# Graph attention over 16 batches on one core: a plan with separate steps for two early tables, the long rows, the pieces and the last batch

## Chip, cores, metric

One core of one Trainium2 chip. The metric is the device time of one execution in microseconds (us); lower is better. "Span" is the time from the first to the last instruction of the one execution that was profiled.

## The reference, cut to what matters

```python
# x: (16, 1024, 512); adj: (1024, 1024), 0/1, ones on the diagonal; biases are zero
h = jnp.maximum(_layernorm(x, axis=-1), 0.0)
q, k, v = (h @ W + b for each of Wq, Wk, Wv)      # 8 heads of 64
scores = einsum('bihd,bjhd->bhij', q, k) / 8 + where(adj == 0, -1e9, 0)
out = einsum('bhij,bjhd->bihd', softmax(scores), v)
return x + out.reshape(b, n, 512)
```

The adjacency matrix is sparse and the same for all batches. The rows have very different numbers of neighbours: many in the first rows, few in the last.

## The kernel before

The kernel sorts the rows by their number of neighbours, so that tile 7 (the last 128 rows in that order) needs only 2 gathered rows per row and tile 0 needs 11 or more. Rows of tile 0 that have still more get extra rows, "pieces" of four neighbours. For each batch it

- loads x in sorted order (an indirect load on GpSimd), normalises (VectorE, GpSimd, ScalarE), transposes and projects it (TensorE), and stores K and V as a table in DRAM;
- gathers rows of K and V in "units" of 2 to 4 (indirect loads on GpSimd; the row's own K and V on SyncE), multiplies them with the queries and sums each head (VectorE), takes the exponential and weighs V (ScalarE), and folds (VectorE, GpSimd) or accumulates (TensorE).

Batch 0 has a **prologue** ahead of it that makes the permutation ("perm"), the lists of neighbours and the slots. The order of all instructions is fixed before the kernel is built: every operation is entered in a plan with an engine, an estimated length and a "place" (a priority), and a list scheduler simulates the engines and buffers and writes down the order it finds. A place is therefore not a position. What comes out depends on everything that is in the plan.

```python
# the prologue in the plan: one table carries the permutation, the norms' scales and the lists
for t in range(NT):
    add(("list_of", t), "DVE", 2.5, -43.18 + t, [("ends",), ("no_diagonal", t)], [sources])
    add(("spread", t), "POOL", 1.35, -40 + t, [("list_of", t), ("shift", (t - NT) // 2)], delay=2.5)
add(("collect",), "SP", 0.05, -31, [("spread", t) for t in range(NT)], delay=3.0)
add(("perm_of",), "DVE", 0.2, -31, [("collect",)])
add(("spots",), "DVE", 2.1, -25, [("collect",)])
add(("long_rows",), "POOL", 1.35, -23.08, [("perm_of",)], [("g", -2)], 4.5, 1.5)
add(("longest", -1), "DVE", 1.25, -4, [("long_rows",)], [sources, ("g", -2)])
for k in range(ROUNDS):
    add(("longest", k), "DVE", 2.5, -0.28 + 0.5 * k, [("longest", k - 1)], [("g", -2)])
add(("pieces",), "DVE", 9.0, 2.19, [("longest", ROUNDS - 1)], [("pht", "pieces"), ("g", -2)], delay=1.0)
add(("slots", 0), "DVE", 0.7, 5, [("pieces",), ("spots",)])
# ... cut: x, norms, projections, stores; then for each unit i of all batches:
    add(slot, "POOL", 1.35, i - 4.33 + 0.1 * s, stored, [g], delay=4.0, moves=1.5)      # gather
    add(("multiply", i), "DVE", 0.15 + 0.533 * count, i, slots + [q_of[q]], [g, q])
    add(("score", i), "DVE", 0.15 + 0.533 * count, i - 0.31, [("multiply", i)], [g])
    add(("exponent", i), "ACT", 0.22, i + 0.15, [("score", i)])
# ... cut

def spread(t):                      # eight scatters into one DRAM tile
    nc.gpsimd.indirect_dma_start(
        out=table[:], out_offset=on(ap=spot_i[:, t : t + 1], axis=0), in_=before[:, t, :], in_offset=None
    )

def longest(k):                     # eight more neighbours per round, always over 1024 columns
    row = LONG[0][:, 0, :]
    # ... cut: two passes that mark the neighbours, for k < 0
    nc.vector.max(found0[:, ts(k, 8)], row)
    if k < ROUNDS - 1:
        nc.vector.match_replace(row, found0[:, ts(k, 8)], row, 0.0)

def slots(later):                   # indices for the gathers, and how many slots are free
    c = slice(split, SLOTS) if later else slice(0, split)
    nc.vector.tensor_scalar(index[:, c], spot[:, c], -1.0, float(N), op0=ALU.mult, op1=ALU.add)
    free = once.tile([P, SLOTS], F32, tag="free", name=f"free_{later}")
    nc.vector.tensor_scalar(free[:, c], spot[:, c], 0.0, -1.0, op0=ALU.is_equal, op1=ALU.mult)
    for t in range(1, NT) if later else (-1, 0):
        # ... cut: first, end
        number = once.tile([P, 1], F32, tag="number", name=f"number_{t}")
        nc.vector.tensor_reduce(number, free[:, first:end], AX.X, ALU.add)
        nc.vector.tensor_copy(weights[:, end, :], number.to_broadcast([P, H]))
    # ... cut

# after main_path: the check of all row sums, in a pool that is opened behind the last output
with tc.tile_pool(name="c_sb", bufs=1) as pool:
    all_rows_fine(tc, pool, sums, cover, fine)
```

## Time and profile before

| | kernel before |
|---|---|
| time: the 3 runs known to the prediction; these and a fourth, in the rounds with the changed one | 1815.95 to 1825.46, median 1818.92; 1809.92 to 1825.46, median 1817.43 |
| span of the profiled execution, mean granted clock | 1806.0 us, 0.959 |
| first multiply of batch 0, of batch 1, of batch 15 | 112.3, 244.0, 1704.8 us |
| beat: (1704.8 - 244.0) / 14 | 104.3 us a batch |
| first multiply of batch 15 to the end | 101.2 us |

The three numbers "first multiply of batch 1", "beat" and "last batch" cut the span into prologue with batch 0, pipeline and tail: 244.0 + 14 x 104.34 + 101.2 = 1806.0. The times are the starts of VectorE's first K times Q product of a batch, read from the timeline.

This is the timeline of ScalarE in the prologue of the kernel before (start, length in us, engine, line, operation, in brackets how long it sat idle and what ended that):

```profile
114.93 0.58 ACT L610 COPY hT<-pht 128x512 f32<-128x512 f32 x1 [16.02 <-remote]
119.19 0.58 ACT L610 COPY hT<-pht 128x512 f32<-128x512 f32 x1 [3.68 <-remote]
```

ScalarE copies transposes (pht) that TensorE has made. TensorE's transposes ended at about 101 us by the trace, and ScalarE starts at 114.9. "Remote" means that the view found no instruction that released it.

### The profile page before, as it was taken

What the parts mean: (1) busy time and instruction counts of PE and PEld (TensorE: products, weight loads), DVE (VectorE), ACT (ScalarE), POOL (GpSimd) and SP (SyncE); (2) the same over time, 40 slices, a digit from 0 to 9 for tenths busy, and PEclk for the clock granted to TensorE, in tenths of its full rate; (3) what the DMA queues carried; (4) which work ended last, traced back from release to release, by engine and by line L of the source; (5) the groups of instructions that cost most, each with busy time, mean ns of one, the idle gap of its engine ahead of it and who ended that gap; (6) DMA issues with size and microseconds to landing.
All of it is one profiled execution on the core that took longest, in us unless ns stands there. A gap on an engine that the chain in (4) does not pass through costs nothing. (4 is left out here: it accounts for less than half of the span.)

```text
span 1806.0 us, 19695 instructions
## 1 busy us (share of the span) xinstructions
PE 1643.0 (91%) x4301; PEld 756.7 (42%) x4301; DVE 1560.5 (86%) x1883; ACT 1495.7 (83%) x5557; POOL 1322.7 (73%) x1230
## 2 busy tenths in 40 slices
PE   6959899898999989899999989899898989999895
PEld 3424344443444444444444444344444444444331
DVE  5567888989889898989889898988988998898995
ACT  4236988998898889988889988989898899889964
POOL 4445668878787887778688777878777777877773
PEclk9969989999999999999999999999999999999997
DMA  5375888889898888989889898988889898998983
GB/s 210 115 260 189 315 301 305 321 292 340 294 350 308 310 323 297 335 303 335 300 317 330 293 332 293 337 322 318 318 302 324 299 333 311 323 337 294 331 308 134
DMA packets 151781, 539.97 MB, mean 299 GB/s; under 512 B 18908, under 2 KB 18908, under 8 KB 151656
## 3 DMA queue, kind: packets, MB, share of 16 engines
q0 software_dynamic: 111888, 399.09, 61.4%
q1 hardware_dynamic: 39768, 139.56, 21.5%
q8 instruction: 36, 0.59, 0.1%
q14 instruction: 89, 0.73, 0.1%
HBM read 437.85 MB, written 100.72 MB: 298 GB/s over the span
## 5 line engine op out<-in xcount | busy, mean ns | idle before, releaser
L829 ACT ACTIVATE g<-g,weights 128x64 f32<-128x64 f32 x4768 | 1181.1, 338 | 15.6 <-DVE weights L816 6.9
L793 POOL DMA_INDIRECT g<-kv,index x624 | 631.7, 1012 | 208.2 <-issue 154.1
L615 PE MATMUL pq<-wq,hT 128*128 128x512 f32 x1024 | 463.8, 596 | 0.0
L615 PE MATMUL pk<-wk,hT 128*128 128x512 f32 x960 | 443.5, 605 | 11.5 <-ACT hT L610 9.2
L803 DVE TENSOR_TENSOR g<-g,pq 128x2048 f32<-128x2048 f32 (+2 forms) x208 | 397.8, 1913 | 39.3 <-PE pq L615 19.0
L615 PE MATMUL pv<-wv,hT 128*128 128x512 f32 x960 | 431.6, 592 | 0.0
L807 DVE TENSOR_REDUCE weights<-g 128x32 f32<-128x2048 f32 (+2 forms) x224 | 430.9, 1924 | 0.7
L834 DVE TENSOR_TENSOR g<-g 128x512 f32<-128x512 f32 (+1 forms) x285 | 286.5, 1009 | 20.9 <-ACT g L829 17.4
L615 PEld LDWEIGHTS pq<-wq,hT 128*128 128x128 f32 x1024 | 196.0, 191 | 225.9 <-issue 222.0
L615 PEld LDWEIGHTS pk<-wk,hT 128*128 128x128 f32 x960 | 186.1, 195 | 231.4 <-issue 203.5
L615 PEld LDWEIGHTS pv<-wv,hT 128*128 128x128 f32 x960 | 182.4, 190 | 214.4 <-issue 211.3
L896 POOL DMA_INDIRECT out_dram<-x,perm x128 | 149.3, 1167 | 97.8 <-DMA out_dram<-x,perm 46.1
L563 POOL DMA_INDIRECT x<-in_x_dram,perm x128 | 145.9, 1140 | 39.5 <-issue 31.0
L852 PE MATMUL acc<-g,ident 128*128 128x512 f32 x176 | 102.4, 699 | 70.2 <-POOL g L834 63.7
L834 POOL TENSOR_TENSOR g<-g 128x512 f32<-128x512 f32 x105 | 139.8, 1331 | 31.9 <-DVE g L834 15.4
L598 ACT ACTIVATE h<-x,shift,rstd 128x512 f32<-128x512 f32 x120 | 91.0, 805 | 46.5 <-DVE shift L588 42.0
L605 PE MATMUL pht<-ident,h 128*128 128x128 f32 x512 | 88.5, 314 | 40.2 <-issue 20.4
L626 ACT COPY kvt<-pk 128x512 f32<-128x512 f32 x120 | 69.0, 575 | 59.4 <-issue 21.2
L823 DVE TENSOR_TENSOR g<-g,weights 128x512 f32<-128x512 f32 (+1 forms) x149 | 108.5, 728 | 1.3 <-issue 0.9
L605 PEld LDWEIGHTS pht<-ident,h 128*128 128x128 f32 x512 | 70.9, 165 | 85.3 <-issue 44.5
L893 POOL TENSOR_TENSOR x<-x,o 128x512 f32<-128x512 f32 x68 | 87.7, 1290 | 24.2 <-DVE o L884 22.0
L610 ACT COPY hT<-pht 128x512 f32<-128x512 f32 x128 | 72.1, 578 | 37.6 <-remote 19.7
(221 smaller groups left out, 1161.7 us busy)
## 6 DMA issues: line engine op xcount, KB each, us to landing
g<-kv SPq DMA_DIRECT2D x128, 512.0 KB
kv<-kvt SPq DMA_DIRECT2D x120, 512.0 KB
g<-kv,index POOLq DMA_INDIRECT x624
adj<-in_adj_dram SPq DMA_DIRECT2D x8, 512.0 KB
x_first<-in_x_dram SPq DMA_DIRECT2D x8, 256.0 KB
x<-in_x_dram,perm POOLq DMA_INDIRECT x128
out_dram<-x,perm POOLq DMA_INDIRECT x128
wk<-in_L_gnn_Wk_dram SPq DMA_DIRECT2D x1, 1024.0 KB
```

The costliest lines, as they stand in the source:

```text
L563: nc.gpsimd.indirect_dma_start(out=X[n][:], out_offset=None, in_=x_rows, in_offset=on(ap=perm[:, t : t + 1], axis=0), element_offset=b * N * D
L598: nc.scalar.activation(HN[n], X[n], AF.Relu, bias=shift, scale=scale)
L605: nc.tensor.transpose(PH[n][:, c, :], hn[:, ts(c, P)], ident)
L615: nc.tensor.matmul(pt, HT[n][:, c, :], W[name][:, c, :], start=False, stop=(c == DC - 1))
L793: nc.gpsimd.indirect_dma_start(out=G[i][:, s].rearrange("p j d -> p (j d)"), out_offset=None, in_=KV[b % len(KV)][:], in_offset=on(ap=inde ...
L803: nc.vector.tensor_tensor(k, k, Q[b, t][:, None, :].to_broadcast([P, count, D]), ALU.mult)
L807: nc.vector.tensor_reduce(weights[:, w, :], heads(G[i][:, :count, 0, :]), AX.X, ALU.add)
L823: nc.vector.tensor_tensor(v, v, own.to_broadcast([P, n, H, HD]), ALU.mult)
L829: nc.scalar.activation(v[:, h, :], v[:, h, :], AF.Identity, scale=weights[:, c + s, h : h + 1])
L834: engine.tensor_tensor(v[:, 0:n], v[:, 0:n], v[:, first : first + n], ALU.add)
L852: nc.tensor.matmul(ACC[b, home], owner_t if t < 0 else ident, v[:, s, :], start=(u == parts_of(home)[0] and s == 0), stop=(u == parts_of(h ...
L896: nc.gpsimd.indirect_dma_start(out=out_rows, out_offset=on(ap=perm[:, t : t + 1], axis=0), in_=X.pop(b * NT + NT - 1 - t)[:], in_offset=No ...
```

## The change

The intent, part by part: the permutation and the norms' scales leave in a small table of their own ("told"), ahead of the lists, and each of the two tables is split over two DRAM tiles in turn, so that a scatter no longer waits for the one just before it; long rows are searched in 16 blocks of 64 columns and only the best of each block in rounds; the pieces become eight operations that the plan can place one by one; all places and lengths are set anew; the last batch runs from tile 0 to tile 7; the check gets tiles of its own, so that it need not wait for the pipeline's.

```diff
-        add(("spread", t), "POOL", 1.35, -40 + t, [("list_of", t), ("shift", (t - NT) // 2)], delay=2.5)
-    add(("collect",), "SP", 0.05, -31, [("spread", t) for t in range(NT)], delay=3.0)
+        behind = lambda name: [(name, t - 2)] if t > 1 else [("zeros",)]
+        add(("tell", t), "POOL", 1.3, -35.76 + 0.3 * t, [("ranks",), ("shift", (t - NT) // 2)] + behind("tell"), delay=2.0)
+        add(("spread", t), "POOL", 1.3, -36.45 + t, [("list_of", t)] + behind("spread"), delay=2.0)
+    add(("collect", "told"), "SP", 0.05, -39, [("tell", t) for t in range(NT)], delay=2.6)
+    add(("collect", "lists"), "SP", 0.05, -31, [("spread", t) for t in range(NT)], delay=2.6)
... (cut: loads reordered, x before the adjacency; count_pieces ... pieces as plan operations)
-        add(("norm", n), "ACT", 0.81, p - 4.41, [("shift", n // 2) if b else ("load_x", n)], [("x", n), ("h", n)])
-        add(("flip", n), "PE", 0.50, p - 4.02, [("norm", n)], [("h", n), ("pht", n)])
+        add(("norm", n), "ACT", 0.81, p - 5.50, [("shift", n // 2) if b else ("load_x", n)], [("x", n), ("h", n)], delay=0.00)
+        add(("flip", n), "PE", 0.62, p - 4.32, [("norm", n)], [("h", n), ("pht", n)])
... (cut: some forty places and lengths of this kind)
+        i = b * NU + (LAST_ORDER.index(u) if b == B - 1 else u)
...
-            add(("add_up", i), "PE", 0.88 * (1 if folds(b, B, count) else count), i + 0.33, weighed, [g, acc])
+            add(("add_up", k), "PE", 0.88 * (1 if folds(b, B, t, count) else count), i + 0.84, weighed + ([("add_up", k - 1)] if u != parts[0] else []), [g, acc])
...
+        def scatter(name, t):
+            nc.gpsimd.indirect_dma_start(
+                out=tables[name][t % 2][:], out_offset=on(ap=spot_i[:, t : t + 1], axis=0), in_=before[name][:, t, :], in_offset=None
+            )
...
+            for c in range(4 * k - 4, 4 * k):
+                block = row.rearrange("p (k c) -> p c k", c=blocks)[:, c, :]
+                got = LONG[0][:, 1, most * c : most * (c + 1)]
+                nc.vector.max(got[:, 0:8], block)
+                nc.vector.match_replace(block, got[:, 0:8], block, 0.0)
+                nc.vector.max(got[:, 8:16], block)
...
-    with tc.tile_pool(name="c_sb", bufs=1) as pool:
-        all_rows_fine(tc, pool, sums, cover, fine)
+    all_rows_fine(tc, keep, sums, cover, fine)
```

## The prediction

> **What bounds the kernel now.** I read the busy table by stage first, because an average over stages with different limits says little. Stage table of the kernel before (stretch, its length, busy us and instruction count of each engine, granted clock, DMA share, GB/s):
>
> ```profile
> 75.00:100.00 25.00, 21.46 (x58) 10.32 (x57) 16.10 (x39) 8.35 (x13) 16.62 (x17) 0.86 0.60 195
> 100.00:125.00 25.00, 4.42 (x23) 3.50 (x22) 17.60 (x27) 5.17 (x8) 13.49 (x15) 0.60 0.97 373
> ...
> 400.00:800.00 400.00, 375.87 (x991) 172.56 (x990) 361.19 (x418) 356.59 (x1347) 312.03 (x285) 0.98 0.88 319
> ```
>
> There are three stages. From about 240 us to 1700 us the sixteen batches run as a pipeline in which four things are nearly full: TensorE 94%, VectorE 90%, ScalarE 89%, DMA 88%. Before that lies a prologue in which almost nothing is full. From 100 to 125 us TensorE works 4.4 of 25 us. After it lies a tail. The start times of the first multiply of each batch (the K times Q product, VectorE L803), read from the timeline, give the beat: batch 1 starts at 244.0 us, batch 15 at 1704.8, so one batch takes (1704.8-244.0)/14 = 104.3 us. Batch 0 starts at 112.3 and so takes 131.7, over 27 us more than a normal one.
>
> Next, the list of waits (waiting instruction, who released it, total us, times, longest):
>
> ```profile
> PE acc L852 <- POOL g L834: 64.1, 16, 8.1
> ...
> DVE sums L874 <- ACT weights L811: 52.6, 33, 13.8
> ...
> DVE g L803 <- PE pq L615: 19.0, 30, 1.9
> ```
>
> In the pipeline TensorE stops once a batch for some 4 us at the first accumulation of tile 0, waiting for the fold on GpSimd. VectorE stops for row sums whose exponentials are not there, and at the first multiply, whose query projection stands behind a K projection. In the stretch 655 to 1596 us, nine batches, VectorE is busy 93.8 us of a batch (mean of five batches) and waits some 10.6: sums 2.5, pq 1.7, shift 1.9, o 1.3, gathered and loaded rows 1.5, others. TensorE is busy 99.5 us. So neither is full: they wait for each other in turn, by a fixed order.
>
> Third, the timeline of the prologue:
>
> ```profile
> 65.78 1.23 DVE L662 MAX8 before<-adj 128x8 f32<-128x1024 f32 x1
> 80.58 0.17 DVE L673 CAST perm<-after 128x8 int32<-128x8 f32 x1 [13.57 <-DMA after<-table]
> ...
> 131.75 0.18 DVE L874 TENSOR_REDUCE sums<-weights 128x8 f32<-128x24 f32 x1 [13.84 <-ACT weights L811]
> ```
>
> VectorE is done with the lists at 67 us and sits idle 13.6 us until the permutation arrives. The cause is on GpSimd: eight scatters into one table, each 2.88 us after the last (61.33 to 75.72 in five steps), though issuing one takes 0.96. With the permutation at 80.6 the loads of x start, the last K/V store goes out at 93.13, the first gathers at 98.2 and 99.45. The second gap, 13.84 us, follows 16.0 and 3.7 us in which ScalarE waited for TensorE's transposes; the view names no releaser ("remote"), and I can't say what it is.
>
> Last, the chain that ended last (start, us, what):
>
> ```profile
> 1793.79 2.75 DMA out_dram<-x,perm
> ...
> 1796.71 1.22 DVE c_both L1025
> 1797.93 1.13 DVE c_both L1026
> ```
>
> The final check begins only when the last output has landed; it runs to 1800.26, and the span ends at 1806.0.
>
> **What the Trainium skill says.** "DMA: Bandwidth & Descriptors", section "Anatomy of one DMA", gives each transfer on the GpSimd path about 2 us of fixed cost, mostly the receipt of the write. The trace agrees: 2.88 us per dependent scatter less 0.96 of issue leaves 1.92. "VectorE: DVE Perf Modes", section on the TRN2 errata, gives a one-input-rate fp32 operation (N+151)/0.96 ns. The trace agrees: 1024 wide 1.22 to 1.23 us against 1.22, 512 wide 0.68 to 0.69. "TensorE: Matmul & The Clock Gate", section "The HAM clock gate", says an idle TensorE falls to half clock; the trace shows 0.60 in 100-125 us. "Perfetto Trace Analysis", section "Identifying the Most-Contended Engine", warns that matmul busy share is no measure of headroom; I therefore don't read 94% as a floor.
>
> **The change, part by part.**
> 1. Two early tables in alternating DRAM tiles. The permutation no longer travels with the lists. Its eight scatters need only the ranks (44.3 us before) and the norms' scales. In the instruction order of the changed kernel they are mixed with K/V stores and the first four lists: sixteen GpSimd issues up to the last one, of which the fourth list is the latest to be ready. Lists start at about 47 us (before 47.8; transposes of the keys come some 2.5 us sooner since x tiles 0 and 1 are loaded and normalised first; one extra 1.2 us operation is put before the lists). Fourth list 47+4x2.39 = 56.6, then two or three issues of 1.25: last scatter about 59.5, landed 61.5, read back at 64.5. On VectorE the permutation stands after the eighth list, about 66.3. So the permutation comes at about 66.8 instead of 80.6: 14 us sooner. But K/V of batch 0 needs 16 projections of 3.65 us on TensorE, which was busy throughout (last one ended at 84.7) and starts only 2.5 us sooner: 82.5 to 84. What is won here is the delay behind it: eviction was at 88.7 because ScalarE stood at a norm whose x came late, and the store at 93.1. Now eviction and store can go at about 84.5, then three x loads, first gathers at about 89. That is 10 us, not 14.
> 2. Long rows by blocks. Before: two passes, ten MAX8 of 1.22, nine replacements of 1.30 = 26.4 us of VectorE, the last at 149.6. After: one pass of 1.23, sixteen blocks of three 64-wide operations, 0.22 us each by the formula plus 0.08 for the value load, 0.74 a block = 11.9, then nine rounds on 256 wide, 0.42 twice and 0.08 = about 8. About 21 us, an estimate: only 5 us less work. The gain is in place: the buffer of the long row is free at about 100 us and not at 153, where the gathers of unit 5 (152.7) waited.
> 3. Pieces as separate operations. Before, one block from 153.2 to 160.5 with waits of 3.8 and 0.7 us of VectorE for TensorE, and slots at 166.5. After, they lie before the first multiply. Worth about 5 us.
> Together: first multiply at about 101 (before 112.3), first exponential at about 104 (before 131.5), the second batch at about 104+107 = 211 (before 244), 33 us sooner at best. The unnamed 16 us wait may come back, as the same transposes and norms alternate; I give it half a chance of 10 to 12 us. Prologue: -27.
> 4. The new places in the pipeline. The set of instructions per batch stays (109 on VectorE in both orders). But on TensorE the first two query projections now come right after the transposes of the next batch, ahead of the K projection; from the tile 0 accumulation to a ready query it was 0.9+0.15+1.2+0.8+3.65+3.65 = 10.3 us, now 5.9. Row sums of VectorE stand one or two operations later, scales' shifts get more distance. That addresses pq 1.7, sums 2.5, shift 1.9 of the 10.6 us of waits; I take half, 3 us of a batch. TensorE's busy 99.5 includes overlap of issue, its work is 24x3.65+4.4+0.9+3.8 = 96.7, so 101.3 is possible. 14 to 15 batches: -43.
> 5. Last batch from tile 0 to 7, check apart. From the last score to landed output was 1784.8 to 1796.5 = 11.8 us (12 accumulations on TensorE, scale, residual). With the two-row unit last: exponential, sums, share 0.9, weighing 2.0, fold 0.7, residual on VectorE 0.7, output 3.1 = 7.4. The check's 3.6 us now run beside the output. Tail: -7.
> Sum: 1818.9-27-43-7 = 1742.
>
> **The rivals.** (a) The pipeline keeps its beat, because it is held by transfers or TensorE. For it: DMA share is 0.88 and would be 0.91, all engines are within 5%. Against: in 1650-1750 us DMA ran at 0.92 to 0.93 and 331 GB/s. Then only 34 us come, 1785. (b) The earlier permutation makes x loads, eight more scatters, and gathers collide: DMA is at 0.97 in 100-125 us already. Then the gathers start earlier but land as late, batch 0 gains 10 rather than 27: 1759 with the rest. (c) TensorE becomes the bound and the waits on it grow: period stays at 103, sum 1765. (d) The unnamed wait vanishes and VectorE's waits mostly go, period 99.5: 1705.
>
> **Range and chances.** The prologue may give 10 to 35, the beat 0 to 70 (weight on 25 to 55), the tail 4 to 9. That gives 1742 with 1705 to 1785. Two per cent is 1782.5, reached if prologue and tail come in full even with hardly any gain in the beat. Faster 0.91, same 0.08, slower 0.01.
>
> **What would show it right or wrong.** The cast of the permutation near 67 us; the first indexed gather near 89; the first exponential near 104; the second batch's first multiply near 211; distance between batches 101 to 102 us; waits of VectorE on sums and pq well under 52.6 and 19.0; the check's reductions over before the last output has landed. The step most likely to be wrong is the beat: if the distance is still 104, the order was not what held it. Next is the 16 us wait of ScalarE.

## More of the kernel before

Kernels that were sent together ran on one chip and share the runs of the kernel before. I call the three groups of experiments **chip A** (kernel before: median 1804.95 us), **chip B** (1814.89) and **chip C** (1793.94). Which chip the first pair of profiles came from is not recorded.

## The result, and the profile after

| | before | after |
|---|---|---|
| median of the runs of the same rounds | 1817.43 (4 runs) | 1770.20 (1770.12 to 1773.76, 4 runs) |
| span, clock | 1806.0, 0.959 | 1768.2, 0.971 |
| first multiply of batch 0 | 112.3 | 128.1 |
| first multiply of batch 1 | 244.0 | 234.6 |
| beat | 104.3 | (1675.0 - 234.6) / 14 = 102.9 |
| last batch to the end | 101.2 | 93.2 |

The ratio of after to before is 0.9744 (95% interval 0.970 to 0.979). A ratio is the mean time of one kernel's fast runs over that of the other's of the same rounds, so it is not quite the ratio of the medians in the table. The change is faster; I had predicted 1742 (-77 us) and it is 1770 (-47). The time is inside the range, and some 30 us of the expected gain are missing. By the cut of the spans, the prologue gave -9.4 where I wrote -27, the pipeline 14 x -1.46 = -20 where I wrote -43, and the tail -8.0 where I wrote -7. These add up to -37.8, the difference of the spans; the medians differ by 47, since the profiled execution of before was a quick one for its kernel (1807.72 us).

One thing in this cut is not like for like: the changed kernel starts its last batch with tile 0, so "first multiply of batch 15" is another instruction in it, and the step from batch 14 to 15 took 101.4 us before and 105.6 after. Over batches 1 to 14, where it is the same instruction, the beat fell from 104.6 to 102.7 us, and from the first multiply of batch 14 to the end it was 202.5 us before and 198.7 after. So the tables here give some 4 us too little to the pipeline and too much to the tail.

The stage table after, to be held against the one in the prediction:

```profile
75.00:100.00 25.00, 14.82 (x36) 6.81 (x34) 6.83 (x33) 3.85 (x6) 18.95 (x20) 0.73 0.80 261
100.00:125.00 25.00, 9.00 (x28) 5.17 (x29) 19.19 (x84) 7.40 (x12) 0.43 (x1) 0.65 0.38 152
400.00:800.00 400.00, 379.92 (x998) 173.82 (x1013) 363.31 (x426) 361.52 (x1363) 316.92 (x289) 0.99 0.89 321
```

In 75 to 100 us VectorE (third pair) worked 6.8 of 25 us, less than before, although its input was there earlier. In 100 to 125 us GpSimd did almost nothing: one instruction. In the pipeline all four engines are a little fuller.

VectorE's waits after (waiting instruction, releaser, total us, times, longest):

```profile
DVE sums L947 <- ACT weights L884: 30.2, 14, 2.4
...
DVE g L876 <- DMA g<-kv,index: 20.3, 16, 2.2
DVE st L599 <- DMA x<-in_x_dram,perm: 19.4, 10, 3.9
DVE g L876 <- PE pq L642: 12.8, 14, 2.2
```

The waits that the new order aimed at are down: row sums from 52.6 (13.8 of it one wait in the prologue) to 30.2, queries from 19.0 to 12.8. The waits for gathered rows and loaded x, 11.0 and 8.7 in the same view before, are now 20.3 and 19.4.

The timeline of VectorE in the prologue, two lines before and then after:

```profile
81.33 0.18 DVE L741 TENSOR_SCALAR index<-spot 128x39 int32<-128x39 f32 x1
...
84.28 0.23 DVE L749 COPY weights<-number 128x8 f32<-128x8 f32 x1
```

```profile
72.10 0.28 DVE L715 CAST perm<-after_told 128x8 int32<-128x8 f32 x1
...
83.12 0.65 DVE L721 COPY spot<-after_lists 128x8 f32<-128x8 f32 x7
89.96 0.18 DVE L814 TENSOR_SCALAR index<-spot 128x39 int32<-128x39 f32 x1 [6.19 <-remote]
...
92.82 0.16 DVE L821 TENSOR_REDUCE number<-free 128x1 f32<-128x8 f32 x1 [2.35 <-remote]
94.26 0.17 DVE L822 COPY weights<-number 128x8 f32<-128x8 f32 x1 [1.28 <-issue]
...
128.12 1.21 DVE L876 TENSOR_TENSOR g<-g,pq 128x1024 f32<-128x1024 f32 x1
```

This is the surprise. The slot computation is a chain of 16 short operations, each of which needs the one before it. They last 0.16 to 0.4 us each and in the kernel before they ran from 81.3 to 84.5 us. Now the first of them waits 6.2 us, most of the others start 0.7 to 2.8 us apart, and the chain ends at 105.7. The semaphore record shows where the time lies: the last of the seven copies to spot ended at 83.77, and VectorE's own semaphore, for which index waits, was raised at 89.94. In the same stretch ScalarE stands for 5.8 and 10.0 us, and two of five DMA instructions on SyncE take 0.69 to 0.70 us where the others take 0.02 to 0.42. Behind the chain come twelve blocks, the last search and the pieces, all on VectorE, and only then the first multiply. The first gather goes out at 93.3 us (I had 89), and the first exponential comes at 130.7 (I had 104), hardly sooner than the 131.5 before.

The tail after: one line of VectorE's timeline, the last transfer in the chain that ended last (start, us, what), and GpSimd's last line:

```profile
1752.49 1.17 DVE L1098 TENSOR_REDUCE c_both<-sums 128x1 f32<-128x1024 f32 x1
```

```profile
1758.06 2.88 DMA out_dram<-x,perm
```

```profile
1761.71 0.96 POOL L969 DMA_INDIRECT out_dram<-x,perm  x1 [2.52 <-DMA out_dram<-x,perm]
```

The transfer at 1758.06 is the last output but one. GpSimd issued the last one only when that had landed at 1760.9, and by the semaphore record it landed at about 1764.4. The check's two long sums, from 1752.5 to 1754.9, are over some 10 us before that.

### The profile page after: what moved, and what is told of

It reads as the page before. It is cut to its first block, busy times and chain, and to the rows that moved or that the text cites.

```text
span 1768.2 us, 19718 instructions
## 1 busy us (share of the span) xinstructions
PE 1619.3 (92%) x4235; PEld 743.0 (42%) x4297; DVE 1560.0 (88%) x1952; ACT 1494.2 (85%) x5556; POOL 1336.4 (76%) x1236
## 4 chain that ended last, share of the span: by engine, by line
PE 22%; DVE 20%; ACT 19%; POOL 16%; issue 13%; DMA 9%; another core or an unknown queue 1%; POOLq 0%; DVEq 0%; SPq 0%; ACTq 0%
ACT g L902 14%; PE pq L642 10%; DVE weights L880 6%; POOL g L866 5%; DMA g<-kv,index 5%; DVE g L907 5%; PE pk L642 5%; DVE g L876 4%; POOL x L966 3%; PE acc L925 3%; DMA out_dram<-x,perm 3%; ACT h L625 2%; POOL out_dram L969 2%; ACT kvt L653 2%; PE pv L642 2%
## 5 line engine op out<-in xcount | busy, mean ns | idle before, releaser
L866 POOL DMA_INDIRECT g<-kv,index x624 | 655.4, 1050 | 189.0 <-issue 156.9
L642 PE MATMUL pk<-wk,hT 128*128 128x512 f32 x960 | 434.6, 595 | 11.4 <-ACT kvt L653 4.7
L876 DVE TENSOR_TENSOR g<-g,pq 128x2048 f32<-128x2048 f32 (+2 forms) x208 | 396.3, 1911 | 35.3 <-DMA g<-kv,index 20.3
L907 DVE TENSOR_TENSOR g<-g 128x512 f32<-128x512 f32 (+1 forms) x286 | 292.6, 1023 | 13.5 <-ACT g L902 10.9
L969 POOL DMA_INDIRECT out_dram<-x,perm x128 | 134.4, 1050 | 89.7 <-DMA out_dram<-x,perm 44.5
L590 POOL DMA_INDIRECT x<-in_x_dram,perm x128 | 131.5, 1027 | 35.7 <-issue 35.4
L907 POOL TENSOR_TENSOR g<-g 128x512 f32<-128x512 f32 x105 | 134.3, 1279 | 10.1 <-DVE g L907 4.4
L925 PE MATMUL acc<-g,ident 128*128 128x512 f32 x172 | 90.6, 644 | 40.6 <-POOL g L907 37.2
L896 DVE TENSOR_TENSOR g<-g,weights 128x512 f32<-128x512 f32 (+1 forms) x149 | 118.1, 793 | 1.0 <-issue 0.3
L632 PEld LDWEIGHTS pht<-ident,h 128*128 128x128 f32 x512 | 64.5, 153 | 102.7 <-ACT h L625 72.9
L599 DVE BATCH_NORM_STATS2 st<-x 128x6 f32<-128x512 f32 x120 | 81.9, 682 | 19.4 <-DMA x<-in_x_dram,perm 19.4
```

What stands on the lines that cost most here:

```text
L590: nc.gpsimd.indirect_dma_start(out=X[n][:], out_offset=None, in_=x_rows, in_offset=on(ap=perm[:, t : t + 1], axis=0), element_offset=b * N * D
L632: nc.tensor.transpose(PH[n][:, c, :], hn[:, ts(c, P)], ident)
L642: nc.tensor.matmul(pt, HT[n][:, c, :], W[name][:, c, :], start=False, stop=(c == DC - 1))
L866: nc.gpsimd.indirect_dma_start(out=G[i][:, s].rearrange("p j d -> p (j d)"), out_offset=None, in_=KV[b % len(KV)][:], in_offset=on(ap=inde ...
L876: nc.vector.tensor_tensor(k, k, Q[b, t][:, None, :].to_broadcast([P, count, D]), ALU.mult)
L907: engine.tensor_tensor(v[:, 0:n], v[:, 0:n], v[:, first : first + n], ALU.add)
```

## The experiments

My first theory, **S**: while GpSimd issues indirect transfers without a pause, signals that an instruction has finished come late, and the new prologue put a chain that lives on such signals into that stretch. The semaphore record above bears out the first half, that the signals are late; why they are is what the runs ask. Rivals: VectorE itself is slow there or gets its instructions late, whatever runs beside it (**V**); the stretch is an artefact of profiled executions (**P**); a number of outstanding transfers does it, at whatever pace (**B**). For the beat: TensorE holds it (**T**), transfers hold it (**D**), or the engines wait for each other in turn (**W**).

### Chip A: the chain, and what holds the beat

**flat.** Sums first, copies after, so that VectorE waits for its own results 3 times and not 15.

```diff
+            number = once.tile([P, NT + 1], F32, tag="number", name=f"number_{later}")
             for t in range(1, NT) if later else (-1, 0):
-                number = once.tile([P, 1], F32, tag="number", name=f"number_{t}")
-                nc.vector.tensor_reduce(number, free[:, first:end], AX.X, ALU.add)
-                nc.vector.tensor_copy(weights[:, end, :], number.to_broadcast([P, H]))
+                nc.vector.tensor_reduce(number[:, t + 1 : t + 2], free[:, first:end], AX.X, ALU.add)
+            for t in range(1, NT) if later else (-1, 0):
+                nc.vector.tensor_copy(weights[:, end, :], number[:, t + 1 : t + 2].to_broadcast([P, H]))
```

> The changed kernel with one edit: in the slot computation of tiles 1 to 7 the seven sums come first and the seven copies after them, so VectorE waits for its own earlier result 3 times instead of 15. Work and transfers stay. In the changed kernel this chain took from 83.8 to 105.7 us, 22 us for some 4 us of work. Theory S (a completion signal of an engine comes 0.7 to 6 us late while GpSimd issues indirect transfers without a pause, so each wait for an own result costs about 1.4 us): the chain ends near 94, the first multiply of batch 0 comes at about 116 instead of 128, and the time is 1757 to 1762. Theory V (VectorE is slow there whatever it waits for, or its instructions come late): the chain stays at about 20 us, 1767 to 1772. Theory P (the gap is in profiled executions only): the profile gets shorter and the time stays at 1770.

Measured: 1768.47 us (1765.62 to 1770.67, 4 runs; ratio to before 0.979), first multiply at 127.1. The changed kernel itself was not run on this chip; beside its ratio of 0.974 on the first pair's chip that is no gain. The timeline of VectorE:

```profile
91.60 0.54 DVE L821 TENSOR_REDUCE number<-free 128x1 f32<-128x8 f32 x7 [2.52 <-remote]
92.30 0.17 DVE L824 COPY weights<-number 128x8 f32<-128x8 f32 x1 [0.16 <-issue]
93.70 0.17 DVE L824 COPY weights<-number 128x8 f32<-128x8 f32 x1 [1.23 <-remote]
```

The seven sums ran in 0.54 us, all of them. The seven copies, each of which needs one of those sums, still lie 0.7 to 2.1 us apart, to 101. My figure of 94 us was wrong. It was wrong because I had taken the delay as a latency, paid once per wait. What the copies show is a rate: the signals of seven sums that ended together were taken up one after the other. The copies start 1.40, 2.11, 1.39, 0.71, 1.39 and 1.40 us apart, which are whole multiples of about 0.70 us. Shortening the chain of waits does not help; V is not excluded by this run.

**gate.** The x loads of batch 0 read a second copy of the permutation that VectorE makes after the slot computation.

```diff
+            nc.vector.tensor_copy(perm_x, after["told"][:, :, own])      # behind slots(1)
-                ... in_offset=on(ap=perm[:, t : t + 1], axis=0), ...
+                ... in_offset=on(ap=(perm if b else perm_x)[:, t : t + 1], axis=0), ...
-            known = [("perm_of",)] if b == 0 else []
+            known = [("spots",)] if b == 0 else []
```

> The changed kernel, but the x loads of batch 0 use a second copy of the permutation that VectorE makes after the slot computation, so that eight to eleven indirect loads less are in flight from 76 to 88 us; everything else as it was. Theory S (late completion signals while indirect transfers are issued densely): the slot computation takes 3 to 5 us instead of 22, x loads start near 88, the first multiply comes at 110 to 116 instead of 128, time 1752 to 1762; the late signals may come back between 88 and 103 and slow the search by blocks. Theory V (VectorE is slow there whatever runs beside it): the slot computation still takes about 20 us, x comes 20 us later as well and the time rises to 1775 or more.

Measured: 1767.42 us (1764.90 to 1774.17, 4 runs; ratio 0.980), first multiply at 125.8. VectorE:

```profile
83.70 0.18 DVE L816 TENSOR_SCALAR index<-spot 128x39 int32<-128x39 f32 x1
...
86.59 0.17 DVE L824 COPY weights<-number 128x8 f32<-128x8 f32 x1
...
108.20 0.43 DVE L751 MAX8 found<-adj_long 128x8 f32<-128x256 f32 x1 [1.86 <-remote]
```

The same 16 operations now take 3.1 us, so V falls: VectorE is not slow by itself. Here its semaphore was raised at 83.68, 0.02 us after the last copy to spot. Nor did instructions arrive late in the changed kernel: in its profile no packet of the two queues that load instructions (q8, q14) starts between 64.0 and 108.4 us, so what VectorE ran from 84 to 105.7 had been loaded before. But the gaps come back in the last search, 97.6 to 119 us, where the x loads and gathers now run. The stretch followed the loads, and nothing was won.

**less_pe.** No bias product, but for K and V of batch 0 (the biases are zero; the result stays right).

```diff
-            nc.tensor.matmul(pt, chosen, bias[name], start=True, stop=False)
+            if n < 0:
+                nc.tensor.matmul(pt, chosen, bias[name], start=True, stop=False)
... (cut: the first product with the weights starts the sum instead)
```

> The changed kernel without the product that adds the bias, in all 16 batches; the biases are zero, so the result stays right. It takes 24 products of 0.22 to 0.38 us a batch from TensorE, 5 to 9 of its 97 to 99 us. Theory T (TensorE is what holds the beat of 102.9 us): about 97 us a batch, time near 1690. Theory W (the engines wait for each other in turn and for gathered rows, TensorE is not the one limit): at most a third of it, 101 to 103 us a batch, time 1740 to 1770.

**less_dma.** K and V of batches 1 to 15 are not stored and every gather reads the table of batch 0. The result is wrong (relative error 0.195).

```diff
+            if n >= 0:
+                return                       # in store_kv
-                in_=KV[b % len(KV)][:],
+                in_=KV[0][:],                # in gather
```

> The changed kernel with a wrong result on purpose: K and V of batches 1 to 15 are computed but not stored, and all batches gather the rows of the first one. This takes 120 stores of 512 KB, 63 of 540 MB, a ninth of the transfers, from the DMA and leaves the engines' work as it was. Theory D (transfers hold the beat of 102.9 us): about 95 us a batch. Theory W (waits in turn, with late gathers as a part): 100 to 102.5 us a batch, waits of VectorE for gathered rows (20.3 us) go down. If transfers don't matter at all: 102.9.

Both have one timed run, of unknown state. Stage rows of flat (the control on this chip), less_pe and less_dma:

```profile
800.00:1200.00 400.00, 383.65 (x1011) 175.99 (x1010) 364.47 (x426) 361.54 (x1363) 316.38 (x289) 0.98 0.90 323
```

```profile
800.00:1200.00 400.00, 369.86 (x920) 169.45 (x919) 367.15 (x423) 360.97 (x1362) 317.69 (x289) 0.96 0.90 323
```

```profile
800.00:1200.00 400.00, 387.01 (x1026) 178.80 (x1025) 371.95 (x431) 367.02 (x1385) 321.92 (x292) 0.98 0.82 284
```

less_pe: TensorE is busy 14 us less in 400, and nothing else moves; 1768.37 us and a beat of (1670.1 - 229.5) / 14 = 102.9, the same as flat's. T falls: TensorE's 96% busy was no bound at all. less_dma: the DMA share goes from 0.90 to 0.82, the time to 1753.65 and the beat to (1655.2 - 231.5) / 14 = 101.7, so a ninth fewer bytes buy 1.2% of the beat. D falls as the one cause. VectorE's waits for gathered rows fell from 15.8 us in flat to 5.4 over the whole run, so late rows are a part of W.

### Chip B: control, pauses, and single parts of the change in the kernel before

**after_again.** No edit.

> The changed kernel as it is, once more, as the control for the runs beside it. So far one profile shows the slot computation of VectorE stretched over 22 us, and the version with its sums and copies apart shows it stretched over 21 us. If that belongs to the kernel: slot computation 18 us or longer again, first multiply 126 to 129, 1764 to 1771. If it was chance: under 8 us, first multiply near 112 and a shorter run by 12 us or more.

Measured: 1767.30 us (1764.63 to 1771.55, 4 runs) beside 1814.89 before; ratio 0.9752 (0.971 to 0.979). First multiply at 128.1; the slot computation again ends at 105.7. It is not chance.

**pace.** After each of the first eleven x loads GpSimd does some 1.4 us of useless work.

```diff
             )                                # in load_x, behind the indirect load
+            if n < NT + 3:
+                for _ in range(2):
+                    nc.gpsimd.tensor_tensor(pause, pause, pause, ALU.add)
```

> The changed kernel with some 1.4 us of GpSimd work put after each of the first eleven indirect loads of x, so that they are issued every 2.6 us and not every 1.25; the same transfers, none left out, and 15 us later at the end. With these loads held back as a whole the slot computation took 3.1 us and the late signals came back 20 us later, in the last search, when the loads ran. Theory S (completion signals come late because indirect transfers are issued without a pause): slot computation under 6 us, last search under 11 us, first multiply at 112 to 117 (before this edit 128), time 8 to 14 us under the control. Theory B (they come late whenever a number of x loads and gathers are outstanding, at whatever pace): the stretch begins later or lasts longer, first multiply 124 to 135, time within 5 us of the control.

Measured: 1758.53 us (1754.51 to 1763.49, 4 runs; ratio 0.9705, 0.967 to 0.975), so 8.8 us under the control by medians, and no run of the one lies in the range of the other. By the timeline of GpSimd the loads go out at 85.17, 87.61 and, behind a K/V store, 91.37 us. VectorE:

```profile
85.54 0.62 DVE L819 TENSOR_SCALAR index<-spot 128x39 int32<-128x39 f32 x1
...
90.15 0.17 DVE L827 COPY weights<-number 128x8 f32<-128x8 f32 x1
...
117.63 1.21 DVE L881 TENSOR_TENSOR g<-g,pq 128x1024 f32<-128x1024 f32 x1
```

The slot computation takes 4.8 us beside running loads, and the first multiply comes at 117.6 and not at 128.1. Adding idle work to the engine that issues the loads made the kernel faster. On this chip S holds against P: the gain is in the median of all runs, not in the profiled one alone. B, in the form "at whatever pace", gave a wrong forecast; but with the pauses the DMA share from 84 to 100 us is also lower, 0.45 against 0.87 in after_again, so this run can't tell the pace of the issues from the number of transfers under way. The last search took 13 us, not under 11, because two statistics of batch 1 in front of it waited 2.3 us for a late x.

**new_places.** The kernel before, with the new places and lengths for batches 1 to 14 alone.

```diff
+    other = other_places(B)                  # the changed kernel's loop, as a table
+    for i, (key, ...) in enumerate(plan.ops):
+        if key in other and 1 <= batch_of(key) < B - 1:
+            length, place, delay = other[key]
```

> The kernel before with one part of the change: batches 1 to 14 have the places and lengths of the changed plan, so that the order of the instructions inside the pipeline is the new one, while prologue and last batch stay. My prediction gave this part -43 (3 us a batch); the two profiles say 104.3 against 102.9, -20. Expected if the -20 belong to the order: 102.7 to 103.2 us a batch, 17 to 24 us under the kernel before. If the shorter beat came from something else (the prologue's buffers, for one): 104 us a batch and under 6 us won.

Measured: 1799.95 us (6 runs; ratio 0.9928, 0.990 to 0.996), beat (1694.9 - 243.6) / 14 = 103.7. A miss, and a flaw of the experiment: the order that came out differs from the changed kernel's in 49 of 108 rows of VectorE in a batch. With the same places the scheduler found a third order, since one dependency of the changed plan was not there. new_order mends it.

**tail_only.** The kernel before with the last batch from tile 0 to 7 and the check apart, old places.

```diff
+        i = b * NU + (LAST_ORDER.index(u) if b == B - 1 else u)
-    with tc.tile_pool(name="c_sb", bufs=1) as pool:
-        all_rows_fine(tc, pool, sums, cover, fine)
+    all_rows_fine(tc, keep, sums, cover, fine)
... (cut: tile 7 of the last batch folded as in other batches, its residual on VectorE)
```

> The kernel before with the other part: last batch from tile 0 to tile 7 with tile 7 folded as in other batches, its residual on VectorE, and the check in tiles of its own, with the old places otherwise. From the first multiply of the last batch to the end it took 101.2 us before and 93.5 after. Expected: 93 to 96 us there and 5 to 8 us under the kernel before; under 2 us if the output of the last tile sets the end either way.

Measured: 1810.10 us (20 runs; ratio 0.9977, 0.996 to 0.999), -4 to -5 us (the interval allows 1 to 7), just under the expected 5 to 8. From the first multiply of the last batch to the end it took 96.4 us, 4.8 less than in the profile of before; from that of batch 14, the same instruction in both, 198.9 and 202.5, so 3.6 less. Its pipeline has VectorE's old order, so it also serves as the picture of before on this chip. In it VectorE, before it writes an o, waits 8.4 us for GpSimd to add the last o to x; this wait is not in the other list. The wait for the scales (shift) is 9.3 us in it, with 2.8 more that the view can't name, and 11.1 in the other. VectorE's waits over six batches, tail_only and then after_again:

```profile
DVE sums L877 <- ACT weights L814: 18.3, 16, 2.2
DVE g L806 <- PE pq L618: 10.0, 13, 1.8
...
DVE g L806 <- DMA g<-kv,index: 3.0, 4, 0.9
```

```profile
DVE sums L947 <- ACT weights L884: 14.5, 6, 2.4
...
DVE g L876 <- DMA g<-kv,index: 8.4, 7, 1.8
...
DVE g L876 <- PE pq L642: 3.7, 5, 0.8
```

On one and the same chip the three terms are: prologue 245.3 to 234.6 = -10.7; beat 104.6 to 102.55 = 14 x -2.05 = -29; last batch 96.4 to 92.2 = -4.2, on top of the 4 to 5 of tail_only. Together -48, which is what the medians say (1814.89 to 1767.30).

### Chip C: the order by itself, the prologue by itself, and shorter pauses

**old_places.** The changed kernel, batches 1 to 14 with the old places (the same device as in new_places, the other way round).

```diff
+    other = other_places(B)                  # the loop of the kernel before, as a table
+    for i, (key, ...) in enumerate(plan.ops):
+        if key in other and 1 <= batch_of(key) < B - 1:
+            length, place, delay = other[key]
```

> The changed kernel with one part undone: batches 1 to 14 have the old places and lengths; compared instruction by instruction, VectorE then has exactly the order of the kernel before in batches 3, 6, 9 and 12. Prologue, last batch and check are the new ones. If the order alone makes the shorter beat: 104.3 to 104.7 us a batch again, 25 to 30 us over the changed kernel, 1793 to 1800. If the new prologue gives part of it: 103 to 104 us a batch, 1778 to 1792.

Measured: 1784.42 us (1781.25 to 1785.58, 4 runs) beside 1793.94 before; ratio 0.9941 (0.992 to 0.996). Beat (1685.9 - 215.7) / 14 = 105.0. The order is what makes the shorter beat: without it the beat is back (pace8 and pace_half below, with the new order on the same chip, have 103.1 and 102.9). The time is under the expected 1793 to 1800, but so is that of the kernel before on this chip against those on chips A and B. The bigger finding is in the prologue. GpSimd issues loads every 1.25 us (89.34, 90.60, 91.85, 93.10 by its timeline, of which one line is shown), and VectorE runs free:

```profile
91.85 0.95 POOL L727 DMA_INDIRECT x<-in_x_dram,perm  x1 [0.30 <-issue]
```

```profile
83.64 0.32 DVE L951 TENSOR_SCALAR index<-spot 128x39 int32<-128x39 f32 x1
...
86.71 0.17 DVE L959 COPY weights<-number 128x8 f32<-128x8 f32 x1
...
111.42 1.21 DVE L1013 TENSOR_TENSOR g<-g,pq 128x1024 f32<-128x1024 f32 x1
```

**new_order.** new_places with the missing dependency.

```diff
-            add(("add_up", i), "PE", ..., weighed, [g, acc])
+            add(("add_up", i), "PE", ..., weighed + ([("add_up", i - 1)] if u != parts[0] else []), [g, acc])
```

> The kernel before with the new places in batches 1 to 14 and one dependency of the changed plan more (each accumulation of a tile comes after the one before it). The run with the places alone had another order in 49 of 108 instructions of VectorE in a batch, so it tested a third order; with the dependency the order is the changed kernel's from batch 4 on, save 2 rows. If the order alone makes the beat: 102.5 to 103 us a batch, 22 to 29 us under the kernel before. If not: 103.5 or more, as in the run with the places alone.

Measured: 1774.00 us (1772.72 to 1776.78, 4 runs; ratio 0.9886, 0.987 to 0.990), 20 us under the kernel before, a little less than the expected 22 to 29; beat 103.1 over all 14 batches and (1670.9 - 541.0) / 11 = 102.7 from batch 4 on, where the order is the changed kernel's save 2 to 4 rows (103.0 without the step into the last batch, which has the old order). Its prologue is the old one. ScalarE in new_places (chip B) and in new_order (chip C), same prologue instructions:

```profile
115.98 0.58 ACT L749 COPY hT<-pht 128x512 f32<-128x512 f32 x1 [17.77 <-remote]
```

```profile
100.99 1.07 ACT L749 COPY hT<-pht 128x512 f32<-128x512 f32 x2 [2.04 <-PE pht L744]
```

The late signals are not there on chip C, with or without the change.

**pace8** (pauses only for the eight x loads of batch 0) and **pace_half** (half the pause).

```diff
-            if n < NT + 3:
-                for _ in range(2):
+            if n < NT:                       # held against pace
+                for _ in range(2):           # pace8; range(1) in pace_half
```

> As the run with pauses, but only after the eight x loads of batch 0; the three of batch 1 and the gathers come 4 us earlier. In the run with eleven pauses VectorE waited 2.3 us for an x of batch 1 and 2.6 us for its scale ahead of the first multiply. Theory S: the stretch stays away, the two waits shrink, first multiply at 112 to 116, 1750 to 1758. If issues without a pause from 102 us on are early enough to bring the late signals into the last search: 118 to 124, 1758 to 1766.

> As the run before it with half the pause: one piece of 0.65 us after each of the eight x loads, an issue every 1.95 us. It tells whether the late signals go gradually or at a threshold between 1.25 and 2.6 us an issue. Gradually: slot computation 8 to 14 us, first multiply 118 to 123, 1757 to 1765. All gone: slot computation under 6 us, first multiply at 111 to 115, 1748 to 1756. Not at all: as the changed kernel, 1764 to 1771.

Measured: pace8 1757.03 us (1753.51 to 1759.61, 4 runs; ratio 0.979), first multiply 113.8; pace_half 1751.94 us (1750.21 to 1754.53, 4 runs; ratio 0.9768, 0.975 to 0.979), first multiply 112.6, slot computation 85.8 to 90.2. Both numbers lie where theory S wanted them, but they say nothing for it: on this chip old_places ran without late signals and without any pause, at the same DMA share (0.84 from 84 to 100 us) as the changed kernel had with them. As tests of a threshold these two runs are void. pace_half has the lowest time of all runs here; since the changed kernel itself was not run on chip C, it is not shown to beat it there. The version that is shown to beat both kernels on one chip is pace: 1758.5 against 1767.3 and 1814.9 on chip B.

## Why the prediction was right, and where it was not

**The time** was inside the range, which was 80 us wide, and the direction right. Mechanisms that held: the permutation no longer waits for the lists; K/V was evicted at 83.7 (I had 84.5); the waits for row sums and queries fell; the check ran ahead of the last output. Three terms of the sum were mis-sized, in the prologue twice and in the beat once; the tail's term came out right by luck.

**Step 1, "So the permutation comes at about 66.8": it came at 72.1.** I let the lists decide when the eighth small scatter could go. The fourth list was ready at 55.7, even before my 56.6. What decided was GpSimd: from 41.7 us to the last small scatter at 67.7 it issued 16 transfers one after the other, never idle for more than 0.3 us. I had 1.25 us for each; five of them took 1.95 to 2.04 us and not 0.96, and one power between them took 1.75:

```profile
46.13 2.04 POOL L692 DMA_INDIRECT told<-before_told,spot_i  x1 [0.19 <-issue]
...
67.66 0.96 POOL L692 DMA_INDIRECT told<-before_told,spot_i  x1 [0.30 <-issue]
```

So the last small scatter went out 8 us later than my 59.5. Some 3 of these were hidden, since I had the permutation behind the eighth list at 66.3 anyway; 5 us remained. The alternating tiles did their work, and the engine that issues became the limit.

**Steps 1 to 3, "first multiply at about 101": it came at 128.1.** Three parts. 5 us are the permutation. Some 17 us are the late signals: old_places has nearly the same prologue without them and its first multiply is at 111.4. The last 5 us are a sum I never made: I counted the work of the long rows as 21 us (it was 24: 1.23, sixteen blocks of 0.84, and 9.0 for the last search) and did not string it together with lists, slots and pieces, though all of it stands on VectorE ahead of the first multiply. From the long row's arrival to the first multiply that is 33 us on chip C with nothing in its way. Batch 0 then took 106.5 us where I had 110, which gives back 3.5. So batch 1 started at 234.6, not at 211: 5 + 17 + 5 - 3.5 = 23.5.

**"The unnamed 16 us wait may come back", half a chance of 10 to 12 us.** This is the term that failed most. It came back in full, some 17 us, in the changed kernel on chips A and B, only in another place: in VectorE's slots and no longer in ScalarE's copies. It is in all profiles on chips A and B but the one with pauses, with the old prologue and the new, and in neither of the two without pauses on chip C. The medians of the kernel before differ by the same size, 1814.9 on B and 1793.9 on C. So the change neither caused nor cured it: the prologue gained 10.7 us where both sides have it (chip B) and 227.4 - 215.7 = 11.7 where neither has it (new_order against old_places, chip C). Chip A doesn't fit so neatly: all its profiles have the late signals, but its median of the kernel before is 1804.95. The -27 was too large by the vanishing that I had half counted on, and by the 10 us of the two steps above.

**Step 4, "I take half, 3 us of a batch": -43.** That the order held the beat was right; the size was off, and only two of the three waits that it named gave way. On chip B the beat fell by 2.05 us, -29 in all; the first pair of profiles shows -20, or 14 x -1.9 = -27 by batches 1 to 14 alone. VectorE's idle time per batch, from the stage rows of six batches, fell from (629.3 - 557.8) / 6 = 11.9 to (613.4 - 559.5) / 6 = 9.0 us, about the half that I had taken, while its busy time per batch rose from 93.0 to 93.2. But it is not the time that I had meant: the wait for queries went from 1.7 to 0.6 us a batch and row sums from 3.0 to 2.4, while shift hardly changed (2.0 with its unnamed waits, then 1.9) and gathered rows rose from 0.5 to 1.4. Half of the fall in idle time is the 1.4 us a batch of waiting for GpSimd to add an o to x, which step 4 did not aim at; that it went was luck. That a faster VectorE asks for rows sooner would explain the gathered rows; it is not shown. That VectorE's busy time is no constant either is something that "SBUF — State Buffer", section "SBUF: two separate sides", may explain: an operation of VectorE with two SBUF inputs and an instruction of GpSimd that reads SBUF lock one shared port pair, and the second waits. The trace neither confirms nor refutes it. The folds of six batches changed their mean length with the order, but both ways: 1024 wide from 1621 ns in the kernel before to 1281 in after_again, 512 wide from 691 to 855, and their sum stayed (117.4 and 116.7 us). It doesn't show who held the port.

**Rival (c)**, that TensorE becomes the bound, named a time near the measured one (1765), but its mechanism is refuted by less_pe. **Rival (b)** named the prologue's gain of 10 and was right in the number; the DMA was nearly full only at the end (0.99 to 1.04 from 98 to 106 us), and the gathers weren't what the first multiply waited for.

**Tail, step 5:** predicted -7, measured -8.0, but the agreement is luck. I had the way from the last score to the landed output at 7.4 us instead of 11.8. It became longer: the last score ended at 1750.1 and the last output landed at about 1764.4, 14.4 us. The sums and the last weighing stood on VectorE behind work of other tiles and the check, and the residual, done at 1758.3, had to wait until the output before it had landed. What held is the check beside the output: from the last landing to the end it is 3.8 us and was 9.5. So -8.0 is -4.7 before the last score, +2.4 from there to the landing and -5.7 behind it, and the -4.7 come mostly from the cut: batch 15 is counted from another instruction (see the result).

One line of the prediction is misread: GpSimd's transfer at 98.20 is a load of x, so the first gather before is the one at 99.45.

**What stays open.** Why signals come late in the profiles of some chips and not of another, and what in the chip passes them on; only two profiles on chip C are without pauses, so even that the chip decides is not shown. Theory S as I began with it is too simple: issuing without a pause was not enough on chip C. On chip B, with the rest of the program the same, a pause took the effect away. Whether the changed kernel shows it on chip C was not run; from old_places and pace_half I estimate it would take 1750 to 1755 us there. Nor is it shown why five of the scatters took twice their usual time to issue.

## What to carry to other kernels

When a stretch of the profile has several engines waiting for "remote" or for themselves, count it as a cost that can come back elsewhere, and compare profiles of more than one chip before you book its disappearance. Be wary of placing a chain of tiny dependent instructions beside a dense run of transfers: here it grew from 3 to 22 us. Leaving air between the issues can pay even if the air is wasted work, as it did on chip B (8.8 us). Before predicting a first start, write down the whole chain on the engine that has to run it, and count the issues of the engine that feeds it: two of my three errors in the prologue were sums that I had not made. And before you call a term right, check that its parts came out, not only its sum.

## What the Trainium skill lacked or had wrong

- No page that I read tells of a compute engine's completion signals that come late. The runs show 16 short VectorE operations stretched from 3 to 22 us, gaps of 0.6 to 6.2 us, with the semaphore raised 6.2 us after the work had ended and starts on multiples of about 0.70 us, while GpSimd issued an indirect transfer every 1.25 us (DMA share 0.65 to 1.04); gone with a load every 2.4 to 3.8 us; present in profiles on two chips and absent on a third. It would belong to "Perfetto Trace Analysis", where semaphore waits are explained.
- "DMA: Bandwidth & Descriptors", section "Anatomy of one DMA": the 2 us of fixed cost agree (2.88 less 0.96). It doesn't say how much the cost of an issue can vary: GpSimd mostly took 0.94 to 1.0 us to issue an indirect transfer, but in some cases 1.95 to 2.04, and 16 of them were the limit of a chain.
- "VectorE: DVE Perf Modes", section on the TRN2 errata: it gives (N + 151) / 0.96 ns for an fp32 tensor_tensor and no time for MAX8 or MATCH_REPLACE8, for which the prediction used the formula. By the formula 64 columns take 0.22 us; MAX8 took 0.25 to 0.27 and the replacement 0.25. At 256 columns it gives 0.42, and the trace has 0.41 to 0.43.
- "Perfetto Trace Analysis", section "Identifying the Most-Contended Engine", lacks nothing here, and less_pe agrees with it that the busy share of matmuls tells little of the distance to a limit: TensorE at 96% busy lost 14 of 400 us of work and the beat stayed at 102.9 us.
